# Every second tile of x3 in the sigmoid stage turned in 32 by 32 blocks on its way through DRAM

## The chip, the cores and the metric

The kernel runs on one core of a Trainium2 chip. The metric is the device time of one execution in microseconds (us). A core has five engines that run side by side and wait for one another through semaphores: PE (TensorE, matrix products and transposes), DVE (VectorE), ACT (ScalarE), POOL (GpSimd) and SP (SyncE, which here only issues DMAs). Each engine takes its own instructions strictly in the order in which the program wrote them; an engine that waits holds back everything behind it.

## The reference

The input x is 8 sequences of 512 tokens with 1024 features, in float32. Four blocks are added to it in turn:

```python
x = x + attn_a(layernorm(x))   # softmax attention, 32 heads of 32
x = x + ffn(layernorm(x))      # gated dense layer
x = x + attn_b(layernorm(x))   # sigmoid attention, 4 heads of 256, causal
x = x + ffn(layernorm(x))      # the same gated dense layer again

def attn_b(x):                 # Q, K, V are x times a fixed row of signs per head
    attn = where(causal, sigmoid(4 * scale * Q @ K.T), 0)
    return attn @ V

def ffn(x):
    hits = softmax(x @ centroids.T / 0.1) > 0.01      # 64 clusters
    dense = x @ weight.T + bias
    return where(any(hits, 1)[:, None] & any(hits, 0)[assignments][None, :], dense, 0)
```

The gate of `ffn` needs, for every token, 64 logits of the normalized x, and one of its two conditions is a maximum over all 4096 tokens. So all logits of the last `ffn` must be there before its first gated output.

## The kernel before, in words

Tokens are worked on in 32 tiles of 128; each of the 8 sequences has 4 tiles. x1, x2 and x3 are x after the first, second and third block. The products contract over features, so a normalized tile is needed with its features across the 128 partitions, that is turned: xT1, xT2 and xT3. All of these are kept in DRAM, one array per tile. The stages follow one another: softmax attention, first dense layer, sigmoid attention, second dense layer.

The change lies in the sigmoid stage, the loop over `s` from L1531. One step `s` handles one head of one sequence (32 steps) and carries older work along. In the order in which a step is written:

- SP: `load_head(s + 2)` (L1275), four DMAs of 128 KB with the turned x2 of a head; it goes into a ring of three buffers.
- PE: `scores(s)` (L1295, `csc`), 8 products; ACT then makes the sigmoid (L1300, `at`) and POOL masks its four diagonal blocks (L1303).
- PE: `by_token` (L333), the short last product of the logits of a tile two steps older; ACT scales it (L336). At every fourth tile it also puts the cluster softmax of a whole sequence (L357 to L380, mostly DVE, with an Exp on ACT at L361) on the list `held`.
- ACT: `keys(s + 1)` (L1287). SP: `load_x2(s + 4)` (L1484), 512 KB, into a ring of ten buffers.
- PE: the turn of tile `s - 6` (L277), two groups of four 128x128 transposes into PSUM; DVE copies the first half out, ACT the second (L279), and POOL sends the turned tile to xT3 (L1442).
- the norm of tile `t = s - 5`: statistics on DVE (L227, L228, L234), the inverse root on POOL (L235), the store of x3 by POOL's queue (L1467), and the scaling on DVE (L243, writes `n`).
- PE: `values(s - 1)` (L1314, `o`), 10 products, whose four results DVE adds to x2 (L1320).
- PE: `by_cluster` (L325, `logitsT`), 8 products of the turned tile `s - 6`; ACT copies the result (L329).
- `run_held`: whatever is on `held`.
- ACT and POOL: `value` (L240, L1281), the V of a later tile.

The order is written out by hand. A tile thus is normed in step `s`, turned and multiplied with the centroids in step `s + 1`, and its logits are finished in step `s + 2`. The turned tile lies in a pool of two buffers (`T3`); the second dense layer later loads it from xT3.

Another form of the turn is already in the kernel: `block_pieces` (L288). DVE turns each 32 by 32 block in place (L294), and SP sends the result with four DMAs (L300), each of 32 partitions, whose rows of 32 elements (128 bytes) are put where they belong in DRAM. It is used for xT2, and for xT1 during the softmax attention, there with a `fetch` (L854) that reads the turned tile back into SBUF for its logits.

Of the kernel before, what the change touches and what calls it, by code (L numbers as in the profile page):

```python
# [13 lines left out]
F32 = mybir.dt.float32  # L14
# [8 lines left out]
P = 128  # L23
B, S, H = 8, 512, 1024
NT = B * S
NC = H // P
TPB = S // P
NTILE = NT // P
# [5 lines left out]
HEADS_B, HD_B = 4, 256  # L34
# [34 lines left out]
class Filler:  # L69
# [38 lines left out]
    def run(self, count):  # L108

        while self.queue and count:  # L110
            count -= self._run_one() > 0
# [1216 lines left out]
def block_body(tc, long, dr, args, out):  # L1328
    x, xT_in, qkvw, qkvb, ow, ob, bv_q, bv_k, bv_v, wT, fbias, cT, assign = args
    nc = tc.nc  # L1330
# [15 lines left out]
    stage, filler = Stage(tc, cst, small, ps_m), Filler()  # L1346
    hits1 = Clusters(stage, long, lgp, cT_s, "a")
    hits2 = Clusters(stage, long, lgp, cT_s, "b")
# [40 lines left out]
    def keep(t):  # L1389
        return kept[:, 0, t : t + 1], kept[:, 1, t : t + 1]  # L1390
# [33 lines left out]
    xring, npool, Tpool = sb("c_x", 10), sb("c_n3", 2), sb("c_T3", 2)  # L1424
    dense1.xring = xring

    def turned_tile(t, xT_dram):

        st = {}

        def xn():
            if "n" not in st:
                st["n"] = npool.tile([P, H], F32, tag="n3", name=f"n3_{t}")
            return st["n"]

        def xT():
            if "T" not in st:
                st["T"] = Tpool.tile([P, NC, P], F32, tag="T3", name=f"T3_{t}")
            return st["T"]

        def last():
            nc.gpsimd.dma_start(xT_dram[t], st["T"].rearrange("p c t -> p (c t)"))  # L1442

        return xn, xT, last
# [15 lines left out]
            turns.append((scale, stage.block_pieces(xn, xT, dr.xT2[t])))  # L1460
        return turns

    def x3_pieces(t):

        xn, xT, last = turned_tile(t, dr.xT3)
        norm = stage.norm_pieces(lambda: x2[t], xn)
        norm.insert(1, (0.0, lambda: nc.gpsimd.dma_start(dr.x3[t], x2[t])))  # L1467
        later = held.extend if t < NTILE - TPB else None
        return norm, stage.turn_pieces(xn, xT, last, vector=(t < NTILE - TPB - 1)), hits2.pieces(t, xT, later)


    x2, heads, held = {}, B * HEADS_B, []

    def run_held():
        run(enumerate(held))
        held.clear()
# [4 lines left out]
    def load_x2(t):  # L1481
        if t < NTILE:
            x2[t] = xring.tile([P, H], F32, tag="x2", name=f"cx2_{t}")
            nc.sync.dma_start(x2[t], dr.x2[t])  # L1484

    def load_head(s):
        if s < heads:
            sig.load_head(*divmod(s, HEADS_B), dr.xT2)
# [41 lines left out]
    turned, normed, by_token = None, None, []  # L1530
    for s in range(heads + 1):  # L1531
        load_head(s + 2)
        if s < heads:
            sig.scores(*divmod(s, HEADS_B))
        run(by_token)
        by_token = []
        if s + 1 < heads:
            sig.keys(*divmod(s + 1, HEADS_B))
        if s == 0:
            for t in range(2, TPB):  # L1540
                sig.value(t, x2, keep(t))
        elif s == 1:
            run([scale for scale, _ in turns])
        load_x2(s + TPB)
        turned, normed = normed, None
        if turned is not None:
            run(turned[0])
        if s > HEADS_B:
            norm, *normed = x3_pieces(s - HEADS_B - 1)
            run(norm)  # L1550
        if s > 0:
            sig.values(*divmod(s - 1, HEADS_B), x2)
        if turned is not None:
            run(turned[1][:1])
            by_token = turned[1][1:]
        run_held()
        if s in (2, 3):
            run(turns[s - 2][1])
        t = s + TPB - 1
        if TPB <= t < NTILE:  # L1560
            sig.value(t, x2, keep(t))
# [4 lines left out]
    dense2.load_turned(0)  # L1566
    dense2.load_turned(1)
    norm, turn, logits = x3_pieces(NTILE - TPB)
    run(norm)
    dense2.sums(0)  # L1570
    steps = [(by_token, 0), (normed[0], 4)]
    before = normed[1]
    for t in range(NTILE - TPB + 1, NTILE):
        following = x3_pieces(t)
        softmax = [(0.0, run_held)] if t == NTILE - TPB + 2 else []
        steps += [(following[0] + before[:1] + softmax, 2), (turn, 2), (before[1:], 1)]
        before, (_, turn, logits) = logits, following
# [33 lines left out]
@with_exitstack  # L1611
def block_kernel(ctx, tc, x, xT_in, qkvw, qkvb, ow, ob, bv_q, bv_k, bv_v, wT, fbias, cT, assign, out):
    long = ctx.enter_context(tc.tile_pool(name="long", bufs=1))
    dram = ctx.enter_context(tc.tile_pool(name="dram", bufs=1, space=DRAM))
    with tc.manual_schedule():
        block_body(tc, long, Scratch(dram), (x, xT_in, qkvw, qkvb, ow, ob, bv_q, bv_k, bv_v, wT, fbias, cT, assign), out)
# [33 lines left out]
```

## Time and profile before

| | |
|---|---|
| time, median of 3 runs | 3823.99 us (3821.19 to 3825.94) |
| time of the profiled execution | 3821.42 us |
| its span, first to last instruction | 3819.7 us |
| mean granted PE clock | 0.998 |
| PE busy | 3760.0 us (98% of the span) |
| DVE, ACT, POOL busy | 2538.5, 916.4, 598.0 us |
| steady steps of the sigmoid stage | about 3120 to 3403 us from the start, 10.91 us each |

In the lines of a timeline the columns are the start in us from the start of the span, the duration in us, the engine, the line of the kernel, the operation, the tile written and the tiles read, and the number of instructions put together in this row; in brackets stands how long the engine had been idle and who ended that. SPq is SP's DMA queue: the row is the issue of the DMA, and its landing is told apart from it. In a table of windows each row is a stretch of time with the busy time of each engine and the number of its instructions, then PEclk, the clock granted to PE as a share of full speed, the busy share of the DMA engines, and GB/s.

### The profile page before, as it was taken

How to read it: one execution, taken by the hardware profiler on the slowest of the kernel's cores; microseconds unless marked ns; L12 is line 12 of the kernel's file. 1: busy time of each engine (PE TensorE's matmuls, PEld its weight loads, DVE VectorE, ACT ScalarE, POOL GpSimd, SP SyncE). 2: the span in 40 equal slices, each digit the busy share in tenths (PEclk: the TensorE clock that was granted, in tenths of full speed). 3: DMA queues.
4: the chain of work that ended last, by engine and by line, in shares of the span. 5: the costliest groups of instructions: out<-in, count | busy, mean ns of one | idle time of the engine just before them, and what ended most of it. 6: DMA issues, size and time to landing. Idle time of an engine off the chain costs nothing.

```text
span 3819.7 us, 58523 instructions
## 1 busy us (share of the span) xinstructions
PE 3760.0 (98%) x23942; PEld 2087.6 (55%) x23942; DVE 2538.5 (66%) x3495; ACT 916.4 (24%) x996; POOL 598.0 (16%) x585
## 2 busy tenths in 40 slices
PE   8999999999999999999999999998999999999999
PEld 4445555555555555555555555543444467774444
DVE  4767676767667667766866766665788844456556
ACT  1222222222222222222222222222111144430000
POOL 1222111111111111111111111111000045530000
PEclk9999999999999999999999999999999999999999
DMA  5335455645655455465455554356566665553332
GB/s 168 118 120 171 127 145 146 186 138 145 187 144 145 151 173 147 130 188 149 132 172 152 145 146 125 114 156 230 160 176 176 170 186 193 190 187 133 132 132 99
DMA packets 674490, 590.59 MB, mean 155 GB/s; under 512 B 268072, under 2 KB 519984, under 8 KB 674224
## 3 DMA queue, kind: packets, MB, share of 16 engines
q1 hardware_dynamic: 645120, 482.77, 44.4%
q0 software_dynamic: 24784, 88.36, 6.0%
q10 hardware_dynamic: 4320, 15.73, 1.0%
q8 instruction: 190, 3.11, 0.4%
q14 instruction: 76, 0.62, 0.1%
HBM read 452.48 MB, written 134.25 MB: 154 GB/s over the span
## 4 chain that ended last, share of the span: by engine, by line
PE 91%; DVE 6%; DMA 1%; issue 1%; ACT 0%; POOL 0%; SPq 0%; DVEq 0%; ACTq 0%; POOLq 0%
PE mm L556 34%; PE dense L1236 19%; PE sc L901 7%; PE sc L873 7%; PE mm L554 7%; PE av L928 6%; PE csc L1295 4%; PE o L1314 4%; PE logitsT L325 1%; PE sc L904 1%; DVE nmax L874 1%; PE den L940 1%; PE tp L277 1%; DVE sum L917 1%; DVE ln_st L227 1%
## 5 line engine op out<-in xcount | busy, mean ns | idle before, releaser
L874 DVE TENSOR_REDUCE nmax<-sc 128x4 f32<-128x2048 f32 x256 | 586.0, 2289 | 299.7 <-PE sc L873 299.7
L906 ACT ACTIVATE pT<-sc 128x2048 f32<-128x2048 f32 x256 | 480.8, 1878 | 1160.5 <-PE sc L904 1155.5
L915 POOL TENSOR_TENSOR sum<-pT,pT 128x1024 f32<-128x1024 f32 x128 | 304.9, 2405 | 765.2 <-ACT pT L906 723.4
L556 PE MATMUL mm<-xT,w 128*128 128x256 f32 x1716 | 416.4, 388 | 1.6 <-DVE rden L943 1.6
L556 PEld LDWEIGHTS mm<-xT,w 128*128 128x128 f32 x1716 | 312.8, 190 | 125.4 <-issue 35.3
L901 PE MATMUL sc<-qk,qk 32*128 32x512 f32 x2048 | 292.6, 641 | 15.1 <-DVE nmax L874 14.6
L917 DVE TENSOR_TENSOR sum<-sum,pT 128x2048 f32<-128x2048 f32 x128 | 292.0, 2282 | 0.8 <-ACT pT L906 0.8
L873 PE MATMUL sc<-qk,qk 32*128 32x512 f32 x2048 | 291.9, 640 | 0.2
L142 DVE TENSOR_TENSOR u<-dense,u 128x512 f32<-128x512 f32 x223 | 149.2, 686 | 185.4 <-PE dense L1236 168.4
L928 PE MATMUL av<-pT,v 128*32 128x512 f32 x2048 | 246.2, 598 | 0.0
L1236 PE MATMUL dense<-sum,s 128*128 128x512 f32 x512 | 232.1, 594 | 2.6 <-DVE s L1183 2.6
L556 PEld LDWEIGHTS mm<-w,xT 128*128 128x128 f32 x1640 | 192.6, 192 | 51.1 <-issue 41.2
L556 PE MATMUL mm<-s,w 128*128 128x256 f32 x852 | 204.6, 386 | 0.0
L556 PE MATMUL mm<-w,xT 128*128 128x128 f32 x1640 | 204.6, 278 | 0.0
L556 PEld LDWEIGHTS mm<-s,w 128*128 128x128 f32 x852 | 156.9, 190 | 68.2 <-issue 29.3
L144 DVE SCALAR_TENSOR_TENSOR qk<-mm,qkvb_s,qk 128x256 f32<-128x256 f32 x224 | 107.6, 480 | 124.9 <-PE mm L556 83.9
L556 PE MATMUL mm<-ow,ctxT 128*128 128x512 f32 x354 | 176.6, 616 | 0.3 <-DMA ow<-o_T 0.2
L1236 PE MATMUL dense<-wT_s,dT_b 128*128 128x512 f32 x384 | 171.4, 593 | 1.7 <-DMA dT_b<-xT 1.7
L1236 PE MATMUL dense<-wT_s,dT_a 128*128 128x512 f32 x384 | 171.0, 593 | 0.0
L556 PEld LDWEIGHTS mm<-w,s 128*128 128x128 f32 x1344 | 156.7, 192 | 19.4 <-issue 19.4
L556 PE MATMUL mm<-w,s 128*128 128x128 f32 x1344 | 166.8, 277 | 0.0
L1236 PEld LDWEIGHTS dense<-sum,s 128*128 128x128 f32 x512 | 96.4, 190 | 123.4 <-issue 112.3
(244 smaller groups left out, 4932.5 us busy)
## 6 DMA issues: line engine op xcount, KB each, us to landing
w<-in_qkvw SPq DMA_DIRECT2D x252, 256.0 KB, 3.0
ow<-o_T SPq DMA_DIRECT2D x240, 256.0 KB, 3.7
w<-qk_T SPq DMA_DIRECT2D x224, 256.0 KB, 2.7
ow<-in_ow SPq DMA_DIRECT2D x180, 256.0 KB, 3.2
w<-v_T SPq DMA_DIRECT2D x112, 256.0 KB, 2.7
x<-in_x SPq DMA_DIRECT2D x32, 512.0 KB, 4.9
dT_a<-xT SPq DMA_DIRECT2D x32, 512.0 KB, 5.9
x_a<-x SPq DMA_DIRECT2D x32, 512.0 KB, 6.8
```

Of the source, the lines that this page charges most:

```text
L554: nc.tensor.matmul(out[ts(j, HD_A)], lhsT[:, ts(j, HD_A)], rhs, **flags)
L556: nc.tensor.matmul(out, lhsT, rhs, **flags)
L873: nc.tensor.matmul(sc[:, h, :], st["q"][rows, ts(qt, P)], st["k"][rows, :], start=True, stop=True)
L874: nc.vector.tensor_reduce(st["nmax"][:, qt, :], sc, AX.X, ALU.max, negate=True)
L901: nc.tensor.matmul(sc[:, h, :], st["k"][rows, ts(kt, P)], st["q"][rows, :], start=True, stop=False)
L906: nc.scalar.activation(pT, sc, AF.Exp, scale=SCALE_A)
L915: nc.gpsimd.tensor_tensor(st["sum"][:, h, :], st["pT", 0][:, h, :], st["pT", 1][:, h, :], ALU.add)
L917: nc.vector.tensor_tensor(st["sum"], st["sum"], st["pT", kt], ALU.add)
L928: nc.tensor.matmul(st["av"][rows, :], st["v"][:, kt, rows], pT[:, h, :], start=(kt == 0), stop=(kt == TPB - 1))
L1236: nc.tensor.matmul(st["acc"], st["left"][LEFT[k]][:, c, :], self.w[RIGHT[k]][:, c, :], start=(c == 0), stop=(c == half - 1),)
L1295: nc.tensor.matmul(sc[:, AT_OFF[i] : AT_OFF[i] + n], k[:, c, ts(i, P)], xT[:, c, i * P :], start=(c == 0), stop=(c == 1),)
L1314: nc.tensor.matmul(acc[:, j - jj, :], at[:, start : start + P], self.v[b * TPB + i][:, cols], start=(i == 0), stop=(i == j),)
```

## The change

`x3_pieces` gets an argument `blocks`. It is true for odd tiles below 27, that is for 13 of the 32 tiles: 1, 3, ... 25. For these the transposes on PE, the two copies and POOL's store of the turned tile are left out. Instead the block turn and its four sends are put at the end of `held`, to be run at the end of the step that norms the tile; the next step issues a fetch of the whole tile from xT3 where the transposes stood, and its `by_cluster` reads the fetched tile. The turned blocks take one of the two `T3` buffers.

```diff
-    def x3_pieces(t):
+    def x3_pieces(t, blocks=False):
         xn, xT, last = turned_tile(t, dr.xT3)
         norm = stage.norm_pieces(lambda: x2[t], xn)
         norm.insert(1, (0.0, lambda: nc.gpsimd.dma_start(dr.x3[t], x2[t])))
         later = held.extend if t < NTILE - TPB else None
+        if blocks:
+            made = []
+
+            def box():
+                if not made:
+                    made.append(Tpool.tile([P, NC, P], F32, tag="T3", name=f"B3_{t}"))
+                return made[0]
+
+            def fetch():
+                nc.sync.dma_start(xT().rearrange("p c t -> p (c t)"), dr.xT3[t])
+
+            held.extend(what for _, what in stage.block_pieces(xn, box, dr.xT3[t]))
+            return norm, [(0.0, fetch)], hits2.pieces(t, xT, later)
         return norm, stage.turn_pieces(xn, xT, last, vector=(t < NTILE - TPB - 1)), hits2.pieces(t, xT, later)
...
         if s > HEADS_B:
-            norm, *normed = x3_pieces(s - HEADS_B - 1)
+            t = s - HEADS_B - 1
+            norm, *normed = x3_pieces(t, t % 2 == 1 and t < NTILE - TPB - 1)
             run(norm)
```

## The prediction, made before the changed kernel was run

> **What bounds the kernel now.** I read the page first, its busy times and the chain that ended last:
>
> ```profile
> PE 3760.0 (98%) x23942; PEld 2087.6 (55%) x23942; DVE 2538.5 (66%) x3495; ACT 916.4 (24%) x996; POOL 598.0 (16%) x585
> ...
> PE 91%; DVE 6%; DMA 1%; issue 1%; ACT 0%; POOL 0%; SPq 0%; DVEq 0%; ACTq 0%; POOLq 0%
> ```
>
> PE carries the end. Whether that holds in the changed stage is told by the table of windows of two of its steps, the second one with the cluster softmax at its front:
>
> ```profile
> 3206.84:3217.74 10.90, 10.90 (x64) 8.35 (x62) 4.37 (x11) 4.45 (x7) 5.51 (x8) 1.00 0.56 193
> 3217.74:3228.65 10.91, 10.91 (x64) 8.35 (x63) 7.33 (x17) 7.43 (x10) 5.06 (x8) 1.00 0.46 156
> ```
>
> The first busy time is PE's: it has no gap at all, at full clock. DVE, ACT and POOL have 3 us and more to spare in each step, and the DMA engines are half busy. So a microsecond off PE is a microsecond gained, and one of waiting on PE is one lost. The timeline of these steps gives the places:
>
> ```profile
> 3211.43 1.04 PE L277 MATMUL tp<-ident,n 128*128 128x128 f32 x8
> ...
> 3212.31 4.48 PE L1314 MATMUL o<-cn,at 128*128 128x256 f32 x20
> ...
> 3216.81 1.41 DVE L1320 TENSOR_TENSOR cx<-o,cx 128x256 f32<-128x256 f32 x4
> 3217.74 0.30 PEld L1295 LDWEIGHTS csc<-cxT,k 128*128 128x128 f32 x2 [0.17 <-issue]
> ...
> 3223.27 1.29 DVE L380 TENSOR_TENSOR hits_b<-hits_b,some 128x64 f32<-128x64 f32 x1
> ...
> 3227.63 1.09 PE L325 MATMUL logitsT<-T,cT_s 128*64 128x128 f32 x16
> ```
>
> The step that norms a tile is the *sending* step here, the next the *fetching* step; time is counted from the start of the fetching step's scores (3217.74 here). The turn takes 0.88 us of PE (3211.43 to 3212.31). PE comes to the logits of the tile (L325) at 3227.63, which is +9.89.
>
> **What is gained.** 13 tiles lose their turn: 13 x 0.88 = 11.4 us of PE. Also gone are a DVE copy of 0.69 us, an ACT copy of 0.59 us and POOL's store of 0.59 us per tile. PE waits for none of them in these steps, so I count them at nothing; the cover is the spare time above. Without the turn PE comes to L325 at +9.89 - 0.88 = +9.01.
>
> **What is added, and when the data is back.** The same block turn and sends already run at the start of this stage, in the same surroundings:
>
> ```profile
> 3103.47 1.23 DVE L294 STREAM_TRANSPOSE T<-n 128x1024 f32<-128x1024 f32 x1
> ...
> 3104.74 3.00 SPq L300 DMA_DIRECT2D xT<-T  x4
> ...
> 3108.16 2.74 SPq L1275 DMA_DIRECT2D cxT<-xT  x4
> ...
> 3111.06 0.34 SPq L1484 DMA_DIRECT2D cx<-x  x1
> ```
>
> The turn takes 1.23 us, and the first send goes out 0.04 us after it. The four issues take 3.00 us; by the answer for L300 in this window the last starts 2.1 us after the first, and the slowest landed 4.3 us after its issue, so the data is in DRAM up to 6.4 us after the first send. Behind the sends SP has the next head (2.74 us) and the next x2 (0.34 us), exactly as in the changed program: SP is free for the fetch at 3111.40, that is 6.66 us after the first send. A fetch of this size (L854, 512 KB) is in the trace 24 times:
>
> ```profile
> DMA to landing us min/median/max: 3.5/3.9/5.7
> ```
>
> So 6.66 + 3.9 = 10.5 us from the first send to the turned tile. The nearest row of a whole round trip is shorter: in the softmax attention a first send at 901.63 has its fetch issued at 907.38, landing 3.9 later, 9.6 in all, with only one load between. Upper end: 6.7 + 5.7 = 12.4. I take 10.5, since it has the loads of this stage in it.
>
> DVE begins the block turn when the four adds are done, 3216.81 + 1.41 = 3218.22, which is +0.48. Turned at +1.71, first send at +1.75, tile there at +12.25. PE wants it at +9.01: a **wait of 3.2 us**. It falls on seven tiles (1, 3, 7, 11, 15, 19, 23).
>
> In the other six (5, 9, ... 25) `held` already has the cluster softmax, and in the changed program's order the block turn stands behind all eight of its DVE instructions. In the step above these end with L380 at 3224.56, +6.82. Turned at +8.05, sent from +8.1, there at +18.6: a **wait of 9.6 us**. For tile 5 there is no L380 yet, which is 1.3 us less, and for tile 25 it is short (0.22 us in the answer for L380), about 1.1 less. Six tiles: 4 x 9.6 + 8.3 + 8.5 = 55.2 us; seven: 7 x 3.2 = 22.4 us. Together 77.6 us.
>
> **What else stands in the queues.** SP: the sends hold the next head back until +4.75 (+11.1 behind a softmax), so it lands about 6 us later, at +10.7 or +17. Its keys are made in the step after the fetching one, 5.9 us after that step's scores begin, which is +19.2 or +25.6 with the waits above: over 8 us of slack, so nothing. The next x2 has more. The fetch also needs its buffer free: the tile before was read by PE at the end of the sending step and stored by POOL about +0.3; both earlier than +8.4. DVE: the block turn pushes the statistics of the next tile back by at most 1.23 us, less the copy that is gone; they feed a norm that ends before PE is let go. POOL's root and x3 store come earlier by the missing store. Nothing here reaches PE.
>
> **The clock after a wait.** Three windows of the trace before:
>
> ```profile
> 3070.20:3073.60 3.40, 1.46 (x10) 1.01 (x9) 3.37 (x4) 2.01 (x3) 0.59 (x1) 1.00 0.77 234
> 3073.60:3077.00 3.40, 3.40 (x5) 1.34 (x6) 3.33 (x6) 2.71 (x3) 0.56 (x1) 0.50 0.88 294
> 300.00:303.40 3.40, 1.04 (x9) 0.59 (x11) 3.40 (x4) 0.72 (x1) 0.00 (x0) 1.00 0.63 220
> ```
>
> An idle PE of 1.94 us was followed by 3.4 us at half clock, in which PE does 1.7 us less work; after the gap of 2.36 us in the third window the clock stayed at 1.00. The Trainium skill, "TensorE: Matmul & The Clock Gate", Part 1, says that PE falls to half clock after at least one idle window of about 3.4 us, and that these windows run freely. By that rule as it stands the seven short waits of 3.2 us cost nothing more and only the six long ones do: 6 x 1.5 = 9 us (1.5 since the slow window begins partly inside the wait). By the rows an idle share of somewhat over half a window is enough, if it falls into one window; I estimate that four of five short waits do so, at 1.4 us each, 7 x 1.1 = 8 us on top. I take the rows: 17 us.
>
> A second rule speaks against the change: "VectorE: DVE Perf Modes", section "The three transpose paths", warns that a plain DMA that transposes through its strides is 19 times slower than the transposing path when the innermost destination stride is large. 512 KB at the 435 GB/s fabric ceiling that "DMA: Bandwidth & Descriptors", Specifications, gives is 1.2 us, so at 19 times 23 us (an estimate): the waits would grow by some 17 us on each tile, to about +300 us. The rows of L300 measure the very same 128-byte sends at 6.4 us in all. They decide, and the rule is left aside.
>
> **The sum.** -11.4 + 77.6 + 17 = +83 us. The profiled execution took 3821.42 us, with a span of 3819.7; that is 2.6 us under the median and inside the three runs. 3821.4 + 83 = 3904.6, so **3905 us**.
>
> **Rivals.**
>
> *The round trip is hidden.* The fetch stands a step after the sends and the logits at that step's end, so there are some 9 us of cover. It is enough if the tile is back by +9.01, that is 7.3 us after the first send on the short tiles; then only the 11.4 us of PE remain, 3810 us, faster. The shortest round trip in the trace speaks against it (9.6), and behind a softmax, where the first send is at +8.1, 0.9 us would be left. 3%. In between, with the waits just eating the gain, 1%.
>
> *Only the short waits show.* If the block turn came ahead of the softmax's later instructions on DVE (they wait for the Exp on ACT, 1.82 us in the trace), all 13 waits would be of 3.2 us: -11.4 + 13 x 3.2 + 13 x 1.1 = +45, 3866 us. DVE's written order speaks against it. 10%.
>
> *Contention.* The sends fill the DMA engines while the head, x2 and POOL's x3 store go on; at 12.4 us per round trip and a full slow window after each wait: 13 x 1.9 + 6 more, +31 on the sum, 3936 us, and beyond. For it speaks the slowest fetch (5.7). 8%.
>
> *The change doesn't do what it says.* Its order on PE has the eight transposes of each of 13 tiles taken out and nothing else moved, so I give this nothing of its own.
>
> The forecast has 78%; its own range, 3876 (round trip 9.6, no slow clock: -11.4 + 66 = +55) to 3936. The range for 8 in 10 reaches down to the case of short waits and a little over the contention's value: 3864 to 3942. A measurement of this kernel tells about 0.2%, 8 us, from no change. Faster 0.03, same 0.01, slower 0.96.
>
> **What would show it.** In the profile after, L325 should have idle time before it that is ended by a DMA into `T`, on 13 tiles only, seven times about 3 us and six times 8 to 10 us. L277 should have 104 fewer transposes on `n`. L294 in this stage should start right after L1320 on the short tiles and after L380 on the long ones. SP should wait for its sends before the fetch. The granted clock should fall to 0.50 in windows after the waits, and the mean below 0.998. Wrong would be: waits equal on all 13 tiles (the order on DVE misread), no wait on PE (cover misjudged), or waits ended by `k` or `cn` (a queue behind SP).

## The result, and the profile after

The changed kernel took 3962.03 us in the median (3960.32 to 3962.94), beside 3824.14 us before: a ratio of 1.0363, 95% interval 1.0351 to 1.0375. It is slower by 138 us, where +83 had been forecast; the result lies above the range. The new code shifts the lines: the fetch is L1479, the x3 store L1468, the load of x2 L1498.

From the page of the changed kernel, the busy times and the chain that ended last:

```profile
PE 3783.9 (96%) x23838; PEld 2095.8 (53%) x23838; DVE 2544.8 (64%) x3495; ACT 909.9 (23%) x983; POOL 592.7 (15%) x572
...
PE 84%; DVE 7%; DMA 4%; issue 2%; SPq 1%; ACT 1%; POOL 1%; POOLq 0%; ACTq 0%; DVEq 0%
```

PE has 104 instructions fewer (13 tiles of 8 transposes), and yet is busy 23.9 us longer. In the chain DMA has gone from 1% to 4%. The answer for L325 (the product `logitsT`) in this stage tells who stops PE:

```profile
its engine sat idle before it (us, times) until:
  issue: 127.3, 28
  DMA T<-xT: 117.1, 13
```

(The row "issue" is that of the weight loads, which run beside the products.) PE waits for the fetch 13 times, 117.1 us in all. The spans differ by 3960.7 - 3819.7 = 141.0 us; 117.1 of waiting and 23.9 of longer work make 141.0. PE's idle time outside these 13 waits is the same as before, 59.7 us.

A short tile in the timeline (tile 1; its fetching step begins at 3132.30):

```profile
3132.30 4.58 PE L1295 MATMUL csc<-cxT,k 128*128 128x512 f32 x16
...
3132.78 1.23 DVE L294 STREAM_TRANSPOSE B<-n 128x1024 f32<-128x1024 f32 x1
...
3134.05 3.00 SPq L300 DMA_DIRECT2D xT<-B  x4
...
3137.15 2.69 SPq L1275 DMA_DIRECT2D cxT<-xT  x4
...
3139.83 1.00 POOL L1468 DMA_DIRECT2D x<-cx  x1
...
3139.94 0.41 SPq L1498 DMA_DIRECT2D cx<-x  x1
3140.58 0.33 SPq L1479 DMA_DIRECT2D T<-xT  x1
...
3140.96 3.60 SPq L1275 DMA_DIRECT2D cxT<-xT  x4
...
3148.15 1.98 PE L325 MATMUL logitsT<-T,cT_s 128*64 128x128 f32 x16 [6.73 <-DMA T<-xT]
...
3150.06 6.63 PE L1295 MATMUL csc<-cxT,k 128*128 128x512 f32 x16
```

All issues are about where the prediction had them, counted from 3132.30: block turn at +0.48, first send at +1.75, fetch at +8.28. But the fetch is not back until just before 3148.15, about 7.4 us after its issue. Three transfers of 512 KB went out in the 3.5 us before it: a head (from 3137.15), POOL's x3 store (3139.83) and the x2 load (3139.94, landed 6.8 us after its issue). The next head follows right behind it (from 3140.96). The windows show what that does to the DMA engines, and to the clock:

```profile
3140.60:3144.00 3.40, 0.82 (x4) 0.38 (x2) 1.53 (x5) 0.00 (x0) 0.23 (x1) 1.00 0.75 197
3144.00:3147.40 3.40, 0.00 (x0) 0.00 (x0) 0.00 (x0) 0.00 (x0) 0.00 (x0) 0.50 1.02 391
3147.40:3150.80 3.40, 2.65 (x17) 2.11 (x18) 0.00 (x0) 0.58 (x2) 0.00 (x0) 0.50 0.84 260
3150.80:3154.20 3.40, 3.40 (x5) 1.35 (x4) 0.00 (x0) 0.83 (x1) 2.33 (x1) 0.50 0.00 0
3154.20:3157.60 3.40, 3.40 (x23) 2.85 (x22) 0.26 (x1) 0.82 (x1) 0.00 (x0) 1.00 0.00 0
```

In the second row the DMA engines are full (1.02) at 391 GB/s while no engine computes. PE then works through two more rows at half clock (0.50), the one in which it starts again and the one after that: the scores after the wait take 6.63 us in place of 4.58.

A tile behind the cluster softmax (tile 9), same view:

```profile
3264.07 1.29 DVE L380 TENSOR_TENSOR hits_b<-hits_b,some 128x64 f32<-128x64 f32 x1
...
3265.28 1.23 DVE L294 STREAM_TRANSPOSE B<-n 128x1024 f32<-128x1024 f32 x1
...
3266.54 3.02 SPq L300 DMA_DIRECT2D xT<-B  x4
...
3268.78 1.01 POOL L1468 DMA_DIRECT2D x<-cx  x1
...
3269.67 4.23 SPq L1275 DMA_DIRECT2D cxT<-xT  x4
3274.00 0.41 SPq L1498 DMA_DIRECT2D cx<-x  x1
3275.74 0.33 SPq L1479 DMA_DIRECT2D T<-xT  x1
...
3281.05 1.98 PE L325 MATMUL logitsT<-T,cT_s 128*64 128x128 f32 x16 [13.35 <-DMA T<-xT]
```

The block turn stands behind L380, as its order said. Here POOL's store falls into the middle of the sends, SP has to wait for them (1.3 us between 3274.41 and 3275.74), and the fetch goes out 9.2 us after the first send instead of 6.7. The fetch then lands about 5.2 us later, so that from the first send to PE's use this tile takes 14.5 us and the short one above 14.1, beside the 10.5 of the prediction.

### The profile page after: what moved, and what is told of

The parts are those of the page before. It is cut to its first block, busy times and chain, and to the rows that moved or that the text cites. A ratio compares the mean times of both kernels' runs of the same rounds, so it can differ in the third digit from the quotient of the medians.

```text
span 3960.7 us, 58392 instructions
## 1 busy us (share of the span) xinstructions
PE 3783.9 (96%) x23838; PEld 2095.8 (53%) x23838; DVE 2544.8 (64%) x3495; ACT 909.9 (23%) x983; POOL 592.7 (15%) x572
## 4 chain that ended last, share of the span: by engine, by line
PE 84%; DVE 7%; DMA 4%; issue 2%; SPq 1%; ACT 1%; POOL 1%; POOLq 0%; ACTq 0%; DVEq 0%
PE mm L556 32%; PE dense L1236 18%; PE sc L901 7%; PE sc L873 6%; PE mm L554 6%; PE av L928 5%; PE csc L1295 3%; DMA T<-xT 2%; PE logitsT L325 1%; PE sc L904 1%; DVE nmax L874 1%; PE den L940 1%; PE o L1314 1%; DMA xT<-B 1%; DVE sum L917 1%
## 5 line engine op out<-in xcount | busy, mean ns | idle before, releaser
L1295 PE MATMUL csc<-cxT,k 128*128 128x128 f32 (+3 forms) x512 | 166.8, 483 | 1.9 <-ACT k L1287 1.9
```

The source lines that it names most:

```text
L1295: nc.tensor.matmul(sc[:, AT_OFF[i] : AT_OFF[i] + n], k[:, c, ts(i, P)], xT[:, c, i * P :], start=(c == 0), stop=(c == 1),)
```

## The experiments

Each is the changed kernel with the edit shown, unless said otherwise; "before" beside them was 3822.2 us. Two theories stood against each other at first: that the fetch is late because other transfers are in flight with it, or that reading back what was just written is slow in itself. The clock's part was a question of its own. In the edits, `turned[0]` and `normed[0]` hold the pieces of a tile's turn: two for PE's own turn, and only one, the fetch, for a block tile; so a length of 1 means a block tile.

**Block turn ahead of the softmax.**

```diff
-            held.extend(what for _, what in stage.block_pieces(xn, box, dr.xT3[t]))
+            held[:0] = [what for _, what in stage.block_pieces(xn, box, dr.xT3[t])]
```

> The changed kernel with one edit: the block turn and its sends are put ahead of the cluster softmax on the held list, not behind it. Theory (the softmax on DVE makes the six long waits): all 13 waits become alike, about 6.3 us, so six of them shrink by 6 us and a little slow clock goes with them: 3962 - 36 - 5 = about 3921 us. Rival (the long waits come from DMA traffic that meets the sends in those steps, not from DVE's order): the six waits stay above 11 us and the time within 10 us of 3962.

Measured: 3916.90 us, ratio to before 1.0249 (1.0235 to 1.0263). The waits, from the answer for L325:

```profile
  DMA T<-xT: 76.4, 13
```

They are 40.7 us shorter in all, and the long ones have become like the short ones, so DVE's order made them long. 5.9 us a tile remain.

**Fetch ahead of head and x2.** In the fetching step the fetch is issued first:

```diff
+        late_head = normed is not None and len(normed[0]) == 1
+        if late_head:
+            run(normed[0])
         load_head(s + 2)
...
-        if turned is not None:
+        if turned is not None and not late_head:
             run(turned[0])
```

> The changed kernel with one edit: in the fetching step SP issues the fetch ahead of the next head and the next x2, not behind them. Theory (the fetch lands late because it shares the DMA engines with the head, x2 and x3 transfers): the fetch goes out at about +7.4 and lands 4 to 5 us later in place of 7.4, so the short waits fall from 6.4 to about 3 us and the long ones from 12.9 to about 10: 3962 - 39 = about 3920 us. Rival (reading back what was just written is slow by itself): the fetch still takes 7 us to land, only 0.8 us per tile is won, about 3951 us.

Measured: 3906.93 us, ratio 1.0227 (1.0211 to 1.0243), more than expected. The times from issue to landing of the fetch over all 13 tiles, first in the changed kernel, then here (answers for L1479):

```profile
DMA to landing us min/median/max: 3.3/5.7/7.5
```

```profile
DMA to landing us min/median/max: 3.2/3.4/4.8
```

It reads the same data, as freshly written, and lands in 3.4 us. So reading back is not slow, and the rival falls. And in the timeline of the first tile:

```profile
3137.08 0.34 SPq L1479 DMA_DIRECT2D T<-xT  x1
3137.20 1.01 POOL L1468 DMA_DIRECT2D x<-cx  x1
...
3137.47 2.68 SPq L1275 DMA_DIRECT2D cxT<-xT  x4
...
3140.19 0.66 SPq L1498 DMA_DIRECT2D cx<-x  x1
...
3140.91 1.89 PE L325 MATMUL logitsT<-T,cT_s 128*64 128x128 f32 x16 [2.11 <-DMA T<-xT]
```

Here the fetch lands in about 3.7 us, beside 7.4 on this tile in the changed kernel. POOL's store is issued 0.12 us after it and the head 0.39 us after it, and neither holds it up: what matters is what was issued ahead of the fetch. The long waits stay at 8.3 to 10.6 us, since their fetch still has to wait for late sends.

**Both orders at once**, the two diffs above together.

> The changed kernel with both orders changed at once: block turn ahead of the cluster softmax, and fetch ahead of the next head and x2. Theory (what is left is the bare round trip: last send landed 5.5 us after the first, fetch 3.8 us): first send at +1.7, tile there at +11.1, PE there at +9.1: 13 waits of 2.0 us, 26 us, and PE busy some 3 to 5 us more than without slow clock: 3822 - 11 + 26 + 4 = about 3841 us. Rival (the gains of the two edits overlap or the traffic pushes elsewhere): above 3860 us.

Measured: 3849.28 us, ratio 1.0069 (1.0055 to 1.0083). The 13 waits are 27.1 us, that is 2.1 each, as expected for the bare round trip. PE is busy 3762.2 us, 13.6 more than 3760.0 - 11.4; some slow clock is left, more than I had put in (the granted clock falls to 0.50 behind five of the waits, of 2.1 to 3.8 us), and the time is 8 us above the expected one. So even the cheapest form in this place is slower than PE's own turn.

**x3 store later.** In a fetching step POOL's store goes behind the step's last multiply:

```diff
+            store = []
+            if turned is not None and len(turned[0]) == 1:
+                store = [norm.pop(1)]
             run(norm)
...
             sig.value(t, x2, keep(t))
+        if s > HEADS_B:
+            run(store)
```

> The changed kernel with one edit: in a fetching step POOL issues its x3 store behind the step's last multiply, some 7 us later, so that it does not meet the sends or the fetch. Theory (the three transfers that are in flight together share the DMA engines, so taking one away speeds up the other two): the fetch of a short tile lands in about 5.5 us in place of 7.4, on the long tiles the last send lands about 2 us sooner; 13 x 2 us and some slow clock: about 3930 us. Rival (only what stands ahead of the fetch in SP's own queue delays it): within 8 us of 3962.

Measured: 3941.53 us (3935.69 to 3947.33), ratio 1.0314 (1.0300 to 1.0328). The waits fall from 117.1 to 98.1 us, by 19 us where 26 were expected. Tile 1, and the sends and the fetch of tile 9:

```profile
3137.54 0.33 SPq L1479 DMA_DIRECT2D T<-xT  x1
...
3143.40 1.98 PE L325 MATMUL logitsT<-T,cT_s 128*64 128x128 f32 x16 [4.98 <-DMA T<-xT]
```

```profile
3254.74 3.02 SPq L300 DMA_DIRECT2D xT<-B  x4
...
3261.26 0.33 SPq L1479 DMA_DIRECT2D T<-xT  x1
```

On tile 1 the fetch lands in 5.7 us in place of 7.4. On tile 9 it goes out 6.5 us after the first send instead of 9.2, so it was the store that met the sends there; its landing then takes 5.9 us, and the wait is only 2 us shorter. The rival, that only SP's own queue counts, falls too: the store has a part in the crowding, but a smaller one than the order on SP's own queue (20 us of time against 55).

**PE kept busy during the wait.** Products that feed nothing are put ahead of L325 on the block tiles:

```diff
+            if len(turned[0]) == 1:
+                spin = ps_m.tile([P, S], F32, tag="mm", name="spin")
+                n = FILL[1] if (s - 6) % 4 == 1 and s > 8 else FILL[0]
+                for k in range(n):
+                    nc.tensor.matmul(spin, cst.ones, cT_s.rearrange("p c n -> p (c n)"), start=(k == 0), stop=(k == n - 1))
             run(turned[1][:1])
```

> The changed kernel with work put on PE that nothing needs: 14 products of 128x512 (28 on the tiles behind a cluster softmax) ahead of the logits of each block tile, 0.43 us each, so 6.0 and 12.0 us, about as long as the waits. Theory (some 33 us of the loss is PE's half clock after the waits): the waits are filled, the clock stays at 1.00 in the stage, and the kernel gets faster although PE does more: 3962 - 33 + 3 (the last tile's wait is shorter than its filling) = about 3932 us. Rival (the slow clock falls inside the waits and costs nothing): 3962 us or a few us more.

Measured: 4038.93 us, ratio 1.0567. The expectation was mis-sized: a float32 product of 128x512 is two rows in the trace and takes twice what I had put in (28 rows, that is 14 products, in 12.18 us), so the filling was twice as long as the waits. The time still adds up: 3822 - 11 + 7 x 12.2 + 6 x 24.4 = 4043, with no wait left. Half the filling:

```diff
-FILL = (14, 28)
+FILL = (7, 14)
```

> As the filled kernel before, with half the filling: 7 products of 128x512 (14 behind a cluster softmax), since each took 0.87 us on PE (28 rows in 12.18 us), not the 0.43 us of one row; so 6.1 and 12.2 us, the length of the waits. The products feed nothing. Theory (PE's half clock behind the waits is the part of the loss that the waits do not explain, about 33 us): PE never waits long, the clock stays at 1.00, and the time is 3822 - 11 + 7 x 6.1 + 6 x 12.2 + about 3 of waits left = about 3930 us. Rival (the slow clock is inside the waits and costs nothing): about 3962 us.

Measured: 3934.38 us, ratio 1.0294 (1.0278 to 1.0310), at a granted clock of 0.997 instead of 0.980. The kernel does 116 us of useless work on PE (133 products of 0.87 us) and is 28 us faster than without it. The waits left are small:

```profile
  DMA T<-xT: 6.8, 10
```

The sum is 3822 - 11 + 116 + 7 = 3934, without any slow clock. That is the slow clock's price, measured: idle time turned into work of the same length costs nothing, and the work behind it runs at full speed.

**Sends alone.** PE makes every turn; the 13 tiles are sent by SP in blocks in place of POOL's store; no fetch:

```diff
             held.extend(what for _, what in stage.block_pieces(xn, box, dr.xT3[t]))
-            return norm, [(0.0, fetch)], hits2.pieces(t, xT, later)
+            last = None
```

> One part of the change alone: the 13 tiles are turned in blocks and sent by SP, in place of POOL's store, but PE still makes its own turn for the logits and nothing is fetched. Theory (block turn, sends and their traffic cost PE nothing, all of the loss is the wait for the fetch): 3822 us, within 5. Rival (the sends slow down the heads or x2 so that PE waits for them): slower by 10 us or more.

Measured: 3824.05 us, ratio 1.0004 (0.9996 to 1.0013). Block turn, sends, and their place in SP's queue cost nothing that can be seen.

**Logits one step later.** The sends and the fetch stay; a block tile's L325 is moved behind the next step's values. For it `T3` gets a third buffer, and the logits of odd tiles and odd sequences a second one (those lines are left out here):

```diff
+        run(waiting[:1])
+        by_token = waiting[1:]
+        waiting = []
         if turned is not None:
-            run(turned[1][:1])
-            by_token = turned[1][1:]
+            if len(turned[0]) == 1:
+                waiting = turned[1]
+            else:
+                run(turned[1][:1])
+                by_token += turned[1][1:]
```

> The changed kernel with the logits of a block tile moved one step later, behind the next step's values; for it the pool of turned tiles has three buffers and the logits have a second set. The sends and the fetch stay as they are. Theory (all of the loss is PE waiting for the round trip, and the slow clock behind it): no waits, clock 1.00, only the 0.88 us of PE per tile are left: 3824 - 11 = about 3813 us, ratio 0.997. Rival (the sends and the fetch cost by themselves, through DMA or SP, whoever waits): slower than before, or equal.

Measured: 3808.10 us (3807.38 to 3810.77), ratio 0.9964 (0.9952 to 0.9977): faster than both kernels. The fetch has a whole step more, PE never waits for it, and the clock is 0.997. PE in two steps of it:

```profile
3151.15 4.58 PE L1295 MATMUL csc<-cxT,k 128*128 128x512 f32 x16
3155.57 0.55 PE L333 MATMUL logits<-twice,lT_b 128*128 128x64 f32 x4
3155.96 4.54 PE L1314 MATMUL o<-cn,at 128*128 128x256 f32 x20
3160.34 4.48 PE L1295 MATMUL csc<-cxT,k 128*128 128x512 f32 x16
3164.65 1.04 PE L277 MATMUL tp<-ident,n 128*128 128x128 f32 x8
3165.53 4.48 PE L1314 MATMUL o<-cn,at 128*128 128x256 f32 x20
3169.94 1.97 PE L325 MATMUL logitsT<-T,cT_s 128*64 128x128 f32 x32
3171.84 4.37 PE L1295 MATMUL csc<-cxT,k 128*128 128x512 f32 x15
```

From 3151.15 to 3171.84 it is 20.69 us for two steps; before it was 2 x 10.91 = 21.82.

**The frame of that version without the blocks**: PE's own turn on all tiles, odd tiles' logits one step later. Against that version:

```diff
-            norm, *normed = x3_pieces(t, t % 2 == 1 and t < NTILE - TPB - 1)
+            norm, *normed = x3_pieces(t)
...
-            if len(turned[0]) == 1:
+            if s % 2 == 1 and s < 33 - 1:
                 waiting = turned[1]
```

> The version with the logits of odd tiles one step later, but with PE's own turn for every tile and no block turn, sends or fetch: the frame of that version alone. Theory (its gain over before is the turns that PE no longer makes, 11.4 us, and some 2 us that the frame gives by putting two tiles' logits together): 3822 - 2 = about 3820 us. Rival (the frame itself makes most of the gain): 3812 us or less.

Measured: 3830.47 us (3825.06 to 3836.22), ratio 1.0022 (1.0015 to 1.0029). Neither expectation: the frame by itself costs 8 us. The timeline shows where:

```profile
3157.33 0.56 PE L333 MATMUL logits<-twice,lT_b 128*128 128x64 f32 x4
3157.72 0.61 PE L277 MATMUL tp<-ident,n 128*128 128x128 f32 x4
3159.02 0.65 PE L277 MATMUL tp<-ident,n 128*128 128x128 f32 x4 [0.69 <-ACT lg_b L336]
```

The list of PE's waits from 3120 to 3420 us sums them up (us in all, times, longest):

```profile
PE tp L277 <- ACT lg_b L336: 8.2, 12, 0.7
```

Two L333 in a row take two of the three PSUM buffers that the turn needs as well, and its second half waits for ACT: 12 times, 8.2 us in all. In the version with blocks this step has no turn. So beside its own frame that version saves 22 us: 11.4 for the turns, 8 for these waits, and some 3 us that no run accounts for.

**All tiles.** The later version with tiles 0 to 25 turned in blocks, block turn ahead of the softmax:

```diff
-            norm, *normed = x3_pieces(t, t % 2 == 1 and t < NTILE - TPB - 1)
+            norm, *normed = x3_pieces(t, t < NTILE - TPB - 2)
```

> The version with the logits one step later, with 26 tiles turned in blocks instead of 13 (tiles 0 to 25, block turn ahead of the softmax). Theory that the DMA engines have room: 26 x 0.88 = 23 us less PE, 3822 - 23 = about 3799 us. Rival (five transfers of 512 KB and the short rows of the sends in each step of some 10 us fill the DMA engines, which were 0.56 busy before; heads or fetches come late and PE waits): above 3808 us, perhaps slower than before.

Measured: 3818.91 us (3816.14 to 3829.56), ratio 0.9993 (0.9985 to 1.0002), no change. The windows over the steady steps, first with every second tile, then with all:

```profile
3160.00:3370.00 210.00, 210.00 (x1171) 161.73 (x1170) 113.75 (x247) 97.91 (x144) 103.84 (x150) 1.00 0.77 227
```

```profile
3160.00:3380.00 220.00, 206.93 (x1100) 153.37 (x1101) 120.87 (x247) 95.76 (x136) 97.93 (x140) 0.99 0.92 240
```

The DMA engines go from 0.77 to 0.92 busy, and PE is no longer full. The list of waits between 3120 and 3410 us has

```profile
DVE B L294 <- PE logitsT L325: 17.3, 19, 3.1
...
PE logitsT L325 <- DMA T<-xT: 13.8, 15, 2.1
```

PE waits for the fetch again, 15 times and 13.8 us in all, and DVE's block turn waits for L325 to free one of the three `T3` buffers. Whether the DMA engines or these buffers set the limit was not tested; of the two counts tried, every second tile is the faster.

## Why the prediction was wrong

- *The mechanism* held: PE waits 13 times for the fetch, seven short waits (5.3 to 6.7 us) and six long ones (9.2 to 13.4 us), on the tiles that were named, and PE's other idle time did not grow; block turn and sends cost nothing (the sends alone: 1.0004).
- *The gain*: 13 turns of 0.88 us, as counted.
- *The round trip* is the step that failed. I took 6.66 us until the fetch is issued and 3.9 us for its landing, from rows of the softmax attention, where one or two loads go out between the sends and the fetch; here five do, and 1 MB. On the short tiles the issue was right and the landing was 7.1 to 7.5 us where the trace has it, beyond my upper end of 5.7; with the fetch put first it was about 3.7 on most of them. On the long tiles the issue came 8.0 to 9.2 us after the first send, since POOL's store met the sends, and the landing was about 5 us. Waits of 117.1 us instead of 77.6.
- *What I had overlooked* was written in the order I had read. For the head and the x2 load ahead of the fetch I counted the 3 us that SP needs to issue them, but not that much of their 1 MB is still on its way when the fetch goes out (the x2 load took 6.8 us to land). To POOL's x3 store I gave no cost because nobody waits for it. On tile 1 the fetch took 7.4 us behind all three, 5.7 with the store gone, and 3.7 ahead of all three. The next head, right behind the fetch, is no part of this as far as the runs show: with the fetch first a head follows it as closely.
- *The clock* was right in kind and too small: PE's busy time beyond 3760.0 - 11.4 is 35.3 us against 17. I counted at most one slow window after a wait. The rows above show PE working through two after a wait of 6.7 us, since the window in which it starts again is slow as well and the next one still is. Filling the waits gave back 28 us. The Trainium skill ("TensorE: Matmul & The Clock Gate", Part 1) has half clock released only after about 3.4 us of sustained work, which agrees with the 3.4 us row at 0.50 with PE busy throughout.
- *The rivals*: contention, at 8%, was the right one in kind, with 3936 us for it still too low: its round trip of 12.4 us was 14.1 and 14.5 on the two tiles shown. The case of short waits only is the kernel of the first experiment, 3917 us beside the 3866 worked out for it, with waits of 5.9 us in place of 3.2. The hidden round trip failed as worked out: even its cheapest form takes 2.1 us more per tile than there is cover.

The two mis-sized terms make the whole error: 39.5 us of waiting and 18 of clock, 58 us, and the span rose by 141 against 83.

## What to carry to other kernels

Work taken off a full engine and replaced by a trip through DRAM is a gain only if the use comes late enough: here the same trip was 3.6% slower with the use at the end of the next step and 0.4% faster with it one step later. The landing time of a transfer has to be taken from the place in the queue where it will stand, with everything that is issued ahead of it on any queue, also what nobody waits for. On a PE that is always busy, a wait is paid twice, once as itself (117.1 us here) and once as slow clock behind it (35.3 us).

## What the runs showed of the hardware that I had not expected

It mattered what had been issued before the fetch, and not what came close behind it: with POOL's 512 KB store issued 0.12 us after it and a head 0.39 us after it, a fetch that stood ahead of SP's other loads landed in about 3.7 us, while behind them and the store, which was issued 0.75 us before it, it took 7.4.
